# Cross-attention on one core: exponentials turned before the maxima, and the last output step moved to the following round

## The chip, the core and the metric

The kernel runs on one core of one Trainium2 chip. Its time is the device time of one execution in microseconds (us). Three executions of the kernel before took 1427.91, 1429.44 and 1430.26 us; the median is 1429.44 us.

## What is computed

There are 64 items; `x[b]` has 256 rows of 512 features, `c[b]` 256 rows of 384. All numbers are float32.

```python
text_p  = x @ W_text + b_text                      # 256 x 512
audio_p = c @ W_audio + b_audio                    # 256 x 512, also the values V
Q = layer_norm(text_p, g1, beta1)
K = layer_norm(audio_p, g2, beta2)
alpha = softmax(Q @ K.T / sqrt(512))
H = (alpha @ audio_p) @ W_out + b_out
out = layer_norm(H + x, g_out, beta_out)
```

The kernel folds W_audio and W_out into one matrix `wao` at the start, so that the last two products become (alpha @ c) @ wao, and b_audio, W_out and b_out into one row `bao`.

## The kernel before, in words

The program is one long unrolled list; each engine executes its own instructions in the order in which the source issues them, and no scheduler reorders them. The engines wait for each other through semaphores only where one reads or overwrites what another wrote.

**Rounds.** A main loop of 62 rounds (`for b in range(B - 2)`) works on five items at once. In round b, `k2` and `q2` are the projections of item b+2, `at` is the attention of item b, `last` that of b-1, `old` that of b-2 and `settled` that of b-3. A prologue projects items 0 and 1 and prepares the weights; a drain after the loop finishes the last items. 

**Products.** Each product of 256 rows is cut into blocks and computed with fewer block products than usual, at the price of sums. `Thirds` (key projection, and output `o`) makes 15 block products of 172 columns in the banks M, L, TU and N; `Fork` (query projection) makes seven of 256 columns in two banks, of which a part (`q2`) is cleared by `Fork.clear` (VectorE memset, L599) and another set by `Fork.seed` (ScalarE copy, L595). Between groups of products VectorE adds banks to each other (`after_one`, `after_three`, `after_four`, `after_five`, `after_six`: L538 to L561 and helper line L486), and later products wait for that. The sums of the left operands are made by GpSimd: `csum` and `zsum` in `Sides` (L320), `xsum` in `sum_x` (L288 to L291). `Sides.add(n)` issues the next n of its seven sums.

**Attention of an item.** `score` (TensorE, L672), `maxima` (VectorE, L682), `exponentials` (ScalarE, L689), `reciprocals` (VectorE, L699), `divide_e` (ScalarE, L703), `store_e` (to DRAM, L707). A round later `fetch_e` reads the exponentials back as 32x32 squares (four DMAs, L72), and `turn_e` transposes the squares on VectorE into `eT` (L75). `context_one` and `context_two` multiply `eT` by the rows of c (TensorE, L738) into `ps_z1` and `ps_z2`; `copy_one` and `copy_two` (ScalarE, L753 and L756) make `zT` of them, from which GpSimd makes `zsum`, and `o` multiplies by `wao`.

**End of an item.** `leave_plus` (VectorE, L486) adds the banks of `o` and x into the rows `y` (tile `yr`). A round later come `sums` and `deviations` (ScalarE, L782 and L790), the reciprocal deviation `rstd` on GpSimd (L372 and L376), and on VectorE `shift(0)`, `shift(1)` (L897), `settle(0)`, `settle(1)` (L906); `store` (L916) writes the 256 rows out. `shift` and `settle` read two operands from SBUF.

**Queues.** All loads and stores but two are issued by SyncE (SP), in program order; an issue that waits holds up those behind it. The order in a round before: `load_c`, `load_x` of item b+4, `fetch_e`, c rows, x rows, then the stores of q, of `y` (L916) and of k (L448), the fetches of q and k, the store of e.

**VectorE in a round before, from the end of `o`'s `after_four`:** `settle(1)`, `maxima`, `Fork.clear`, `turn_e`, `leave_plus` with `reciprocals` in its midst; then in the next round `after_one`, the turn of c, `after_three` (L543, twice L486), `after_six` (twice L486), `after_four`, `shift(0)`, `after_five` of q, `shift(1)`, `settle(0)`, the end of k, the turns of q and k, `after_one` of `o`, the turn of x, `after_three` and `after_four` of `o`.

Of the kernel before, what the change touches and what calls it, by code (L numbers as in the profile page):

```python
# [9 lines left out]
F32 = mybir.dt.float32  # L10
# [12 lines left out]
def kernel(  # L23
# [56 lines left out]
    def load_c(b):  # L80
        cq = blk.tile([P, S // SQ, DA // NQ], F32, tag="cq", name=f"cq_{b}")
        squares(cq, c[b])
        blocks[b] = [cq]

    def load_x(b):
        xq = blk.tile([P, L // SQ, D // NQ], F32, tag="xq", name=f"xq_{b}")
        squares(xq, x[b])
        blocks[b].append(xq)
# [5 lines left out]
    def load_x_rows(b):  # L94
        x_rows[b] = xin.tile([P, LT, D], F32, tag="x", name=f"x_{b}")
        nc.sync.dma_start(x_rows[b], x[b].rearrange("(t p) d -> p t d", p=P))

    def load_c_rows(b):
        c_rows[b] = cin.tile([P, ST, DA], F32, tag="c", name=f"c_{b}")
        nc.sync.dma_start(c_rows[b], c[b].rearrange("(t p) d -> p t d", p=P))  # L100
# [142 lines left out]
    def fold_bias(part):  # L243

        ps = third[3]
        nc.tensor.matmul(ps, lhsT=ones, rhs=part, start=True, stop=True)
        nc.vector.tensor_copy(bao_sb, ps)

    def moments(mv, src, t):

# [31 lines left out]
    def sum_x(xT):  # L282

        n = DC // 2
        part = lambda i, j: xT[:, j * n : (j + 1) * n, bass.ts(i, P)]
        s = work.tile([P, 4, n, P], F32, tag="xsum", name="xsum")
        add = nc.gpsimd.tensor_tensor
        add(s[:, 0], part(1, 0), part(1, 1), ALU.add)  # L288
        add(s[:, 1], s[:, 0], part(0, 0), ALU.subtract)  # L289
        add(s[:, 2], part(0, 0), part(1, 0), ALU.subtract)  # L290
        add(s[:, 3], part(0, 1), s[:, 1], ALU.subtract)  # L291
        ss = {
            1: part(0, 0), 2: part(0, 1), 4: part(1, 1),
            5: s[:, 0], 6: s[:, 1], 7: s[:, 2], 3: s[:, 3],
        }
        return {p: [ap[:, k, :] for k in range(n)] for p, ap in ss.items()}
# [624 lines left out]
    def turn_x(b):  # L921
        xT = work.tile([P, DC, L], F32, tag="xT", name=f"xT_{b}")
        turn(xT, blocks[b][1], DC)
        return xT
# [63 lines left out]
    k[1].evict(0)  # L988
    k[1].evict(1)
    Fork.clear()  # L990
    bt_step = const.tile([P, H2], F32, tag="bt_step", name="bt_step")
    nc.vector.tensor_tensor(bt_step, bt_sb[:, :H2], bt_sb[:, H2:], ALU.subtract)
    q[0].normalise()
    q[0].store()
    load_c(2)
    q[0].fetch()
    load_x(2)
    xT[1] = turn_x(1)
    Fork.seed()
    k[1].square()  # L1000
    xs[1] = sum_x(xT.pop(1))
# [27 lines left out]
    q[0].turn()  # L1029
    cT[2] = turn_c(2)  # L1030
    cs[2] = Sides(cT.pop(2), "csum").add()
    xT[2] = turn_x(2)
    xs[2] = sum_x(xT.pop(2))
    fold_multiply(2, 2, 4)
    fold_evict(2)
    q[0].affine(g1_sb, be1_sb)
    q[1].five()
    q[1].after_five()
    third_weights(wa_sb, wa_t, [1], nc.vector)
    fold_bias(part)  # L1040
    q[1].rest()
# [11 lines left out]
    def last_rows(b):  # L1053
        x_rows[b] = blk.tile([P, LT, D], F32, tag="xq", name=f"x_{b}")
        nc.sync.dma_start(x_rows[b], x[b].rearrange("(t p) d -> p t d", p=P))
        c_rows[b] = blk.tile([P, ST, DA], F32, tag="cq", name=f"c_{b}")
        nc.sync.dma_start(c_rows[b], c[b].rearrange("(t p) d -> p t d", p=P))

    for b in range(B - 2):
        at = att[b] = att.get(b) or Attention(b)  # L1060
        settled, old, last = att.pop(b - 3, None), att.get(b - 2), att.get(b - 1)
        three = b + 3 < B
        if b + 4 < B:
            load_c(b + 4)
            load_x(b + 4)
        if b > 1:
            last.fetch_e()
            load_c_rows(b)
            load_x_rows(b - 1)
        if not three:  # L1070
            last_rows(B - 2)
            last_rows(B - 1)
        if b == 1:
            go_sb = row(g_out, "go")
            beo_sb = row(beta_out, "beo")
        if b == 0:
            at.score(0, 8)
            Fork.seed()
            Fork.clear()
        k2 = k[b + 2] = Thirds("k", b + 2, cs.pop(b + 2), wa_blocks, ba_sb, ba_delta)  # L1080
        if b < 3:
            q[b + 2] = Fork(b + 2, xs.pop(b + 2), wt_blocks)
        q2 = q[b + 2]
        if settled:
            settled.sums()
        k2.one()
        k2.after_one()
        if b == 1:
            last.reciprocals()
            last.divide_e()  # L1090
            last.store_e()
            last.fetch_e()
            load_c_rows(b)
        k2.two()
        if old:
            old.context_two(0)
            old.context_two(1)
            old.copy_two()
        k2.three()
        if three:  # L1100
            cT[b + 3] = turn_c(b + 3)
        if b:
            at.affine_keys(0, 1)
        k2.after_three()
        if old:
            old.start_products()
        if b < 3:
            q2.one()
            q2.after_one()
        q2.seven()  # L1110
        q2.after_seven()
        if b:
            at.affine_keys(2, 3)
        q2.six()
        q2.after_six()
        if settled:
            settled.deviations()
        if three:
            cs[b + 3] = Sides(cT.pop(b + 3), "csum").add(2)
        k2.four()  # L1120
        k2.after_four()
        if settled:
            settled.shift(0)
        q2.five()
        q2.after_five()
        if settled:
            settled.shift(1)
            settled.settle(0)
        if b:
            at.affine_queries(0, 1)  # L1130
        k2.five()
        k2.after_five()
        k2.leave()
        k2.last_middle()
        if three:
            cs[b + 3].add(3)
        if old:
            old.o.seed()
        elif three:
            k2.seed()  # L1140
        if b:
            at.affine_queries(2, 3)
        q2.rest()
        q2.square()
        q2.scales()
        q[b + 1].turn()
        k[b + 1].turn([0])
        k2.square()
        k2.scales()
        if b:  # L1150
            at.score(0, 2)
        if old:
            old.o.one()
            old.o.after_one()
            old.o.two()
        if three:
            xT[b + 3] = turn_x(b + 3)
        if b:
            at.score(2, 4)
        if old:  # L1160
            old.o.three()
            old.o.after_three()
        k[b + 1].turn([1])
        if b:
            at.score(4, 7)
        if not three:
            att[b + 1] = Attention(b + 1)
            att[b + 1].affine_queries()
        q2.normalise()
        q2.store()  # L1170
        if old:
            old.o.four()
            old.o.after_four()
        if settled:
            settled.settle(1)
            settled.store()
        if b:
            at.score(7, 8)
        if old:
            old.o.five()  # L1180
        if three:
            Fork.seed()
        k2.normalise()
        k2.store()
        q2.fetch()
        k2.fetch()
        if three:
            cs[b + 3].add()
            xs[b + 3] = sum_x(xT.pop(b + 3))
        if b < 2:  # L1190
            wao_blocks = third_weights(wao_sb, wao_t, [b])
        if b == 1:
            last.turn_e()
        at.maxima()
        if three:
            Fork.clear()
        if not three:
            att[b + 1].affine_keys()
        at.exponentials()
        if b > 1:  # L1200
            last.turn_e()
        if three and b > 1:
            q3 = q[b + 3] = Fork(b + 3, xs.pop(b + 3), wt_blocks)
            q3.one()
            q3.after_one()
        if old:
            old.o.leave_plus(x_rows[b - 2], at.reciprocals)
        elif b:
            at.reciprocals()
        if last:  # L1210
            last.context_one()
        if three and old:
            k2.seed()
        if b:
            at.divide_e()
        if three and b:
            at.store_e()
        if last:
            last.copy_one()

    settled, old, last = att[B - 5], att[B - 4], att[B - 3]
    at = att[B - 2]
    load_x_rows(B - 3)
    for t in range(ST):
        old.context_two(t)
    old.copy_two()
# [3 lines left out]
    last.transpose_e(bank[4])  # L1230
    settled.statistics()
    last.copy_e()
    k[B - 1].turn()
    q[B - 1].turn()
    at.maxima()
    at.exponentials()
    at.reciprocals()
    old.o.one()
    old.o.after_one()
    settled.shift(0)  # L1240
    settled.shift(1)
    old.o.two()
    last.context_one()
    last.copy_one()
    old.o.three()
    old.o.after_three()
    for t in range(ST):
        last.context_two(t)
    last.copy_two()
# [102 lines left out]
```

## Time and profile before

| what | value |
|---|---|
| median of three runs | 1429.44 us |
| the profiled execution | 1432.0 us, span of its instructions 1430.2 us, mean granted TensorE clock 0.992 |
| busy share of the span | TensorE 98%, its weight loads 87%, VectorE 84%, ScalarE 77%, GpSimd 71% |
| a round in the middle (605.00 to 626.27 us) | 21.27 us, TensorE busy 21.24, VectorE 18.66, GpSimd 15.73 |
| the first 100 us | TensorE busy 83.78 us |
| 1370 to 1430.2 us | TensorE busy 43.23 us |

Times within the profile are microseconds from the start of the span. PE is TensorE's matmuls, PEld its weight loads (they run beside the matmul before), DVE is VectorE, ACT ScalarE, POOL GpSimd, SPq SyncE's queue. A float32 matmul appears as two instructions with a weight load each. A busy TensorE in the profile is not TensorE at its peak, since the ends of pipelined matmuls are modelled; a short wait is seen better in the distance between starts. A line of the timeline gives start, length, engine, line and tile, and in brackets the idle time of that engine just before with what ended it. A line of the windows gives, for a stretch, its length, then for PE, PEld, DVE, ACT and POOL the busy time with the number of instructions, then the granted clock, the share of DMA and GB/s.

### The profile page before, as it was taken

Reading aid. Unit: us, or ns where it says so; the run is one execution under the profiler, and the core shown is the slowest. Engines: PE = TensorE matmul, PEld = TensorE weight load, DVE = VectorE, ACT = ScalarE, POOL = GpSimd, SP = SyncE. Lnnn points to the kernel's source line nnn. Section 1 sums busy time; section 2 is a strip of 40 time slices with the busy share of each in tenths; the row PEclk is TensorE's granted clock in tenths of the full one; section 3 lists DMA queues with packets and bytes.
Section 4 is the critical chain, followed back from the end, with each engine's and each line's share of the span. In section 5 each row is a group of like instructions: output and inputs, shape, how many; then the busy total and the mean of one; then the engine's idle time right before and its main releaser. Section 6 shows DMA issues by size and latency. Waiting matters only on the chain.

```text
span 1430.2 us, 26034 instructions
## 1 busy us (share of the span) xinstructions
PE 1394.9 (98%) x7423; PEld 1240.5 (87%) x7423; DVE 1203.5 (84%) x2560; ACT 1100.7 (77%) x2814; POOL 1017.9 (71%) x1685
## 2 busy tenths in 40 slices
PE   9789999999999999999999999999999999999986
PEld 4679989999999899899898899898898999999874
DVE  5748888888888888888888988888888888888857
ACT  4558778778788788788787887887878878878863
POOL 3776877877877777777777787787787687777634
PEclk9989999999999999999999999999999999999999
DMA  8587787888788788787878878788878788777651
GB/s 212 144 212 220 226 245 235 228 237 243 231 229 248 233 238 235 233 232 231 242 227 244 234 226 248 232 230 238 240 226 238 244 229 242 236 233 228 209 174 74
DMA packets 449093, 321.99 MB, mean 225 GB/s; under 512 B 153781, under 2 KB 381621, under 8 KB 448950
## 3 DMA queue, kind: packets, MB, share of 16 engines
q1 hardware_dynamic: 448854, 320.20, 77.2%
q8 instruction: 60, 0.98, 0.3%
q14 instruction: 83, 0.68, 0.1%
q10 hardware_dynamic: 96, 0.13, 0.0%
HBM read 203.57 MB, written 116.65 MB: 224 GB/s over the span
## 4 chain that ended last, share of the span: by engine, by line
PE 82%; DMA 5%; POOL 3%; DVE 3%; SPq 2%; ACT 2%; issue 1%; DVEq 0%; ACTq 0%; POOLq 0%
PE ps_f L603 23%; PE ps_m L502 14%; PE ps_sc L672 13%; PE ps_z L738 11%; PE ps_n L502 10%; PE ps_u L502 7%; PE ps_l L502 5%; SPq L72 2%; DMA kd<-kr 2%; DMA xq<-in_x_dram 1%; POOL csum L320 1%; DMA ed<-e 1%; DMA c<-in_ctx_dram 1%; POOL rstd L376 1%; POOL xsum L289 0%
## 5 line engine op out<-in xcount | busy, mean ns | idle before, releaser
L320 POOL TENSOR_TENSOR zsum<-zT 128x256 f32<-128x256 f32 x124 | 73.9, 596 | 284.7 <-ACT zT L756 271.6
L672 PE MATMUL ps_sc<-kT,qT 128*128 128x256 f32 x1024 | 260.9, 379 | 0.5 <-ACT zT L753 0.5
L320 POOL TENSOR_TENSOR zsum<-zsum,zT 128x256 f32<-128x256 f32 x310 | 196.0, 650 | 14.6
L672 PEld LDWEIGHTS ps_sc<-kT,qT 128*128 128x128 f32 x1024 | 186.5, 190 | 17.9 <-ACT zT L753 0.9
L738 PE MATMUL ps_z<-eT,c 128*128 128x256 f32 x768 | 195.0, 391 | 7.0 <-DVE eT L75 5.6
L320 POOL TENSOR_TENSOR csum<-csum,cT 128x256 f32<-128x256 f32 x310 | 192.4, 629 | 9.8
L603 PE MATMUL ps_f<-wtsum,xsum 128*128 128x256 f32 x756 | 186.7, 383 | 0.9 <-POOL xsum L290 0.9
L906 DVE SCALAR_TENSOR_TENSOR yr<-yr,rstd,beo 128x512 f32<-128x512 f32 x124 | 131.4, 1061 | 52.0 <-POOL rstd L376 52.0
L738 PEld LDWEIGHTS ps_z<-eT,c 128*128 128x128 f32 x768 | 139.8, 192 | 36.3 <-DVE eT L75 20.4
L603 PEld LDWEIGHTS ps_f<-wtsum,xsum 128*128 128x128 f32 x756 | 139.3, 192 | 17.1 <-POOL xsum L290 1.7
L376 POOL TENSOR_TENSOR rstd<-ve,nhalf 128x2 f32<-128x2 f32 x192 | 136.4, 710 | 16.0
L477 ACT ACTIVATE kT<-kT,columns 128x256 f32<-128x256 f32 x256 | 139.5, 595 | 0.0
L477 ACT ACTIVATE qT<-qT,columns 128x256 f32<-128x256 f32 x256 | 138.8, 592 | 0.0
L603 PE MATMUL ps_f<-wt,xT 128*128 128x256 f32 x504 | 130.2, 381 | 0.0
L689 ACT ACTIVATE e<-ps_sc,nmx 128x256 f32<-128x256 f32 x128 | 59.6, 470 | 81.1 <-DVE nmx L682 81.1
L897 DVE SCALAR_TENSOR_TENSOR yr<-yr,nm,go 128x512 f32<-128x512 f32 x124 | 103.3, 835 | 0.0
L603 PEld LDWEIGHTS ps_f<-wt,xT 128*128 128x128 f32 x504 | 93.5, 191 | 10.2 <-issue 0.3
L486 DVE TENSOR_TENSOR ps_l<-ps_m,t 128x172 f32<-128x172 f32 x248 | 85.7, 346 | 17.3 <-ACT junk L410 0.5
L782 ACT ACTIVATE junk<-yr 128x512 f32<-128x512 f32 x124 | 77.0, 621 | 28.8 <-DVE yr L486 28.6
L486 DVE TENSOR_TENSOR ps_f<-ps_f,s 128x256 f32<-128x256 f32 x126 | 54.5, 432 | 49.7 <-PE ps_f L603 46.8
L561 ACT COPY kr<-ps_l 128x344 f32<-128x344 f32 x62 | 27.7, 446 | 87.0 <-DVE kr L486 86.7
L790 ACT ACTIVATE junk<-yr,nm 128x512 f32<-128x512 f32 x124 | 87.8, 712 | 0.0
(227 smaller groups left out, 3767.5 us busy)
## 6 DMA issues: line engine op xcount, KB each, us to landing
kd<-kr SPq DMA_DIRECT2D x64, 512.0 KB, 4.1
kq<-kd SPq DMA_DIRECT2D x256, 128.0 KB, 3.3
qd<-qr SPq DMA_DIRECT2D x64, 512.0 KB, 3.0
qq<-qd SPq DMA_DIRECT2D x256, 128.0 KB, 3.4
xq<-in_x_dram SPq DMA_DIRECT2D x252, 128.0 KB, 3.3
x<-in_x_dram SPq DMA_DIRECT2D x63, 512.0 KB, 4.4
out_dram<-yr SPq DMA_DIRECT2D x62, 512.0 KB, 2.8
cq<-in_ctx_dram SPq DMA_DIRECT2D x252, 96.0 KB, 3.5
```

Of the source, the lines that this page charges most:

```text
L320: nc.gpsimd.tensor_tensor(*step)
L376: nc.gpsimd.tensor_tensor(r, ve, nhalf[:, :n], ALU.pow)
L477: nc.scalar.activation(self.T[:, k, :], self.T[:, k, :], AF.Identity, bias=bet[:, k : k + 1], scale=gam[:, k : k + 1],)
L486: nc.vector.tensor_tensor(o, i0, i1, op)
L502: nc.tensor.matmul(place, lhsT=self.sides.of[n], rhs=self.weights[n], start=(n == 14), stop=True, skip_group_check=True,)
L603: nc.tensor.matmul(place, lhsT=side, rhs=w, start=False, stop=True, skip_group_check=True)
L672: nc.tensor.matmul(self.sc[:, t, :], lhsT=self.qT[:, k, bass.ts(t, P)], rhs=self.kT[:, k, :], start=(k == 0), stop=(k == HC - 1),)
L738: nc.tensor.matmul(ps, lhsT=c_rows[self.b][:, s, bass.ts(j, P)], rhs=self.eT[:, s, :], start=(s == 0), stop=(s == ST - 1),)
L782: nc.scalar.activation(junk, self.y[:, t, :], AF.Identity, scale=-1.0 / D, accum_out=self.nm[:, t : t + 1])
L790: nc.scalar.activation(junk, self.y[:, t, :], AF.Square, bias=self.nm[:, t : t + 1], accum_out=self.ssq[:, t : t + 1],)
L897: nc.vector.scalar_tensor_tensor(row, row, self.nm[:, t : t + 1], go_sb, ALU.add, ALU.mult)
L906: nc.vector.scalar_tensor_tensor(self.y[:, t, :], self.y[:, t, :], self.r[t], beo_sb, ALU.mult, ALU.add)
```

## The change

It moves instructions; it adds and removes none but one, a copy that goes to another engine. TensorE's own order is the same in both kernels, and ScalarE's too but for that copy.

- In each round from b = 2 on, `turn_e` stands ahead of `maxima` instead of behind `exponentials`.
- `settle(1)` and the store of `y` leave the end of the round; they come half a round later, in the next round, between `after_seven` and `six` of q (`done` carries the item over). On VectorE `settle(1)` then stands between `after_three` of k and `after_six` of q.
- `fetch_e` and the loads of c rows and x rows move from the head of the round to behind that store.
- Round 0 and 1: `Fork.clear` comes behind `after_one` of k; five instead of two of the sums `csum` come before `four`; in round 1 the store of e goes ahead of the loads of c and x of item 5, and the rows g_out and beta_out are loaded a round later.
- Prologue: `bt_step` behind the turn of x of item 1; the turn and sums of x of item 2 behind `after_five` of q; `bao` copied by ScalarE instead of VectorE.
- Drain: the turns of the last item's k and q go behind `after_three` of `old.o`, `reciprocals` a little later; the last `settle(1)` left over and its store come first.

```diff
@@ fold_bias
-        nc.vector.tensor_copy(bao_sb, ps)
+        nc.scalar.copy(bao_sb, ps)
@@ prologue
-    bt_step = const.tile([P, H2], F32, tag="bt_step", name="bt_step")
-    nc.vector.tensor_tensor(bt_step, bt_sb[:, :H2], bt_sb[:, H2:], ALU.subtract)
     q[0].normalise()
     q[0].store()
     load_c(2)
     q[0].fetch()
     load_x(2)
     xT[1] = turn_x(1)
+    bt_step = const.tile([P, H2], F32, tag="bt_step", name="bt_step")
+    nc.vector.tensor_tensor(bt_step, bt_sb[:, :H2], bt_sb[:, H2:], ALU.subtract)
     Fork.seed()
...
-    xT[2] = turn_x(2)
-    xs[2] = sum_x(xT.pop(2))
     fold_multiply(2, 2, 4)
     fold_evict(2)
     q[0].affine(g1_sb, be1_sb)
     q[1].five()
     q[1].after_five()
+    xT[2] = turn_x(2)
+    xs[2] = sum_x(xT.pop(2))
     third_weights(wa_sb, wa_t, [1], nc.vector)
@@ main loop
+    done = None
     for b in range(B - 2):
...
-        if b + 4 < B:
+        if b + 4 < B and b != 1:
             load_c(b + 4)
             load_x(b + 4)
-        if b > 1:
-            last.fetch_e()
-            load_c_rows(b)
-            load_x_rows(b - 1)
-        if not three:
-            last_rows(B - 2)
-            last_rows(B - 1)
-        if b == 1:
+        if b == 2:
             go_sb = row(g_out, "go")
             beo_sb = row(beta_out, "beo")
         if b == 0:
             at.score(0, 8)
             Fork.seed()
-            Fork.clear()
...
         k2.one()
         k2.after_one()
+        if b < 2:
+            Fork.clear()
         if b == 1:
             last.reciprocals()
             last.divide_e()
             last.store_e()
+            load_c(b + 4)
             last.fetch_e()
             load_c_rows(b)
+            load_x(b + 4)
         k2.two()
...
         q2.after_seven()
         if b:
             at.affine_keys(2, 3)
+        if done:
+            done.settle(1)
+            done.store()
+        done = settled
+        if b > 1:
+            last.fetch_e()
+            load_c_rows(b)
+            load_x_rows(b - 1)
+        if not three:
+            last_rows(B - 2)
+            last_rows(B - 1)
         q2.six()
         q2.after_six()
...
-            cs[b + 3] = Sides(cT.pop(b + 3), "csum").add(2)
+            cs[b + 3] = Sides(cT.pop(b + 3), "csum").add(2 if b > 1 else 5)
...
-            cs[b + 3].add(3)
+            cs[b + 3].add(3 if b > 1 else 0)
...
             old.o.four()
             old.o.after_four()
-        if settled:
-            settled.settle(1)
-            settled.store()
+        if last:
+            last.turn_e()
...
-        if b == 1:
-            last.turn_e()
         at.maxima()
-        if three:
+        if three and b:
             Fork.clear()
...
         at.exponentials()
-        if b > 1:
-            last.turn_e()
@@ drain
     load_x_rows(B - 3)
+    done.settle(1)
+    done.store()
...
     last.copy_e()
-    k[B - 1].turn()
-    q[B - 1].turn()
     at.maxima()
     at.exponentials()
-    at.reciprocals()
     old.o.one()
     old.o.after_one()
     settled.shift(0)
     settled.shift(1)
     old.o.two()
+    at.reciprocals()
     last.context_one()
     last.copy_one()
     old.o.three()
     old.o.after_three()
+    k[B - 1].turn()
+    q[B - 1].turn()
     for t in range(ST):
         last.context_two(t)
```

## The prediction

> **What bounds the kernel now.** I first read the windows, which say how full TensorE is in each stretch. Two of rounds:
>
> ```profile
> 605.00:626.27 21.27, 21.24 (x118) 19.23 (x117) 18.66 (x41) 17.16 (x45) 15.73 (x27) 1.00 0.80 237
> 626.27:647.54 21.27, 21.24 (x118) 19.23 (x117) 18.66 (x41) 17.16 (x45) 15.73 (x27) 1.00 0.82 235
> 116.04:136.93 20.89, 20.89 (x117) 19.20 (x115) 18.21 (x40) 17.08 (x44) 15.35 (x26) 1.00 0.71 199
> ```
>
> TensorE is full in the middle, so little can be had there: yet the first full round takes 20.89 us and the later ones 21.27. It is the one round whose context product finds `eT` ready, because `settle(1)` does not yet stand ahead of `maxima`. The timeline shows the 0.38 us in a later round:
>
> ```profile
> 604.27 0.68 DVE L75 STREAM_TRANSPOSE eT<-eq 128x512 f32<-128x512 f32 x1
> 605.00 1.59 PEld L738 LDWEIGHTS ps_z<-eT,c 128*128 128x128 f32 x8 [0.24 <-DVE eT L75]
> 606.37 0.52 DVE L486 TENSOR_TENSOR yr<-ps_n,n 128x344 f32<-128x344 f32 x1
> 607.00 0.59 PEld L502 LDWEIGHTS ps_n<-wa,csum 128*128 128x128 f32 x4 [0.40 <-issue]
> ```
>
> The context waits for `eT`; then the next key product waits until `leave_plus` has read bank N (606.89), and that is late because the turn of `eT` stood ahead of it. The remaining idle time is at the ends: TensorE works 83.78 of the first 100 us and 43.23 of the last 60. Its waits there, with what stood behind them:
>
> ```profile
> 53.98 0.27 DVE L599 MEMSET ps_f<- 128x256 f32 x1 [3.08 <-ACT qr L652]
> 55.00 0.91 PE L502 MATMUL ps_u<-wa_thirds,csum 128*128 128x172 f32 x2 [2.55 <-DVE ps_u L486]
> 92.77 3.46 PE L738 MATMUL ps_z<-eT,c 128*128 128x256 f32 x8 [5.40 <-DVE eT L75]
> 1386.93 0.91 PE L502 MATMUL ps_u<-wao_thirds,zsum 128*128 128x172 f32 x2 [4.61 <-DVE ps_u L486]
> ```
> ```profile
> 81.87 0.38 SPq L707 DMA_DIRECT2D ed<-e  x1
> 88.57 1.81 SPq L72 DMA_DIRECT2D eq<-ed  x4
> ```
> ```profile
> 1381.97 1.25 DVE L75 STREAM_TRANSPOSE kT<-kq 128x1024 f32<-128x1024 f32 x1 [6.22 <-DMA kq<-kd]
> ```
>
> **The drain.** VectorE waits 6.22 us for `kq`; `maxima` and `after_one`, which frees TensorE, stand behind. With the turns moved, `maxima` runs when the scores end (about 1379.1) and bank T is written at 1380.7, so the product of 1386.93 follows the context directly, at 1382.2: 4.8 us. The granted clock was 0.5 from 1386.0 to 1392.8; the products from 1386.93 to 1392.96 took 6.03 us, at the full-clock pitch of the loop (146 and 216 ns a pass) 3.05. Without the idle time that is 3.0 more. What is late next: both turns (1.25 and 1.20) plus one `settle` (0.74) now stand ahead of `after_four`, which ends near 1387.4, where the next product into M could start at 1385.8: 1.8 back. `settle(1)` at the head is hidden in VectorE's wait for scores. ScalarE's affines (4.1 us) end before they are needed. `kq` should land earlier, as no store precedes that of k; were it as late as before (1381.9), the turns, due at 1383.7, would still not wait. Gain 4.8 + 3.0 - 1.8 = **6.0**, bounds 3 (half clock again) to 7.8 (no 1.8).
>
> **The start.** Round 0: the memset waits for `qr`, `after_one` behind it. Turned round, bank T is ready when VectorE's weight sums end (about 51), and the next wait is that for the query bank's seed (ScalarE, 53.74 to 54.12): the query product starts at 54.2, not 55.71, 1.5. `bt_step` (1.18) behind the turn lets GpSimd's chain, without a pause from 33.46 to the `rstd` of 52.55, start up to 1.1 sooner; `bao` (0.68) goes where ScalarE is idle. I take 2.0, between 1.5 and 2.6. Round 1: the query product at 72.18 waits for squares, `rstd`, `csum`, `xsum` in a row, which stay; the earlier sums and the clear gain nothing: 0. Then the store of e: it was ready at 72.9, but queued behind the fetches of q and k and ten loads. Now it follows the fetch of k, which ends at 76.86, 5.0 earlier, with one load (1.9) before its fetch; even with its landing of 6.7 the fetch is issued by 83.6 rather than 88.57, with the median 3.6 by 80.6. `eT` is then there about 84 to 87, and the scores ended at 87.37: the wait of 5.40 goes, and the half clock behind it (3.46 against 1.73): 7.1. Late next is GpSimd: `wao_thirds` runs to 96.4 and had 2.4 us before `zsum`; with all earlier by nine, `zsum` waits for it. The output product is due 12 us after the context, so this costs 0 to 1.5; I take 0.6. Loads put off (x of item 5, g_out, beta_out) have over 10 us until use. Sum 2.0 + 7.1 - 0.6 = **8.5**, bounds 5 and 11.
>
> **The rounds.** `turn_e` (0.61 from start to start) takes the place of `settle(1)` (0.87): `maxima` 0.26 sooner, `leave_plus` 0.6 more by the turn that no longer stands behind it. Both waits vanish: -0.38, the row of 20.89. The cover of the fetch: it is issued some 0.5 us later or as before, as the k store no longer waits for `y` (603.95 to about 603.05), lands about 620, is turned at 623.7; c and x rows have over 2 us too. Behind `settle(1)` in its new place stand `after_six` and GpSimd's `zsum`. After `after_three` VectorE had 0.63 idle; `settle` needs more, because it meets `zsum`. The price is shown where `settle(0)` meets `csum`:
>
> ```profile
> 615.70 0.73 POOL L320 TENSOR_TENSOR csum<-cT 128x256 f32<-128x256 f32 x1
> 615.77 1.20 DVE L906 SCALAR_TENSOR_TENSOR yr<-yr,rstd,beo 128x512 f32<-128x512 f32 x1 [0.87 <-POOL rstd L376]
> 616.51 1.06 POOL L320 TENSOR_TENSOR csum<-csum,cT 128x256 f32<-128x256 f32 x1
> ```
>
> The later of the two is held until the earlier is nearly done: `settle` ends 0.55 after `csum`, alone it takes 0.74; the next `csum` loses 0.33. In the new place the second `zsum` (610.59) starts 0.11 ahead of `settle` (610.70): the same order. `settle` then takes 1.16, `after_six` ends 0.35 later, the query product behind it is late by 0.14; hidden, because a longer chain comes: `zsum` 0.33 later, `rstd` too, then `settle(0)` (which already waits 0.87 for it), the end of k, the turns, `after_three` of `o` at 622.18, without a gap. That was on TensorE's heels: its load came at 622.24, 0.06 late within the 20.89. So 20.89 + 0.33 = 21.22 against 21.27: **-0.05** a round, 57 rounds, 2.7 us. Bounds: -0.38 (GpSimd had slack I do not see) to +0.53 (below).
>
> The Trainium skill (SBUF — State Buffer, "Who interferes with whom") speaks against this step: a VectorE instruction with two SBUF inputs and a GpSimd one that reads SBUF exclude each other for the whole instruction. By its letter the third `zsum` would lose not the row's 0.33 but some 0.66, and the rounds would cost 0.28 each, 16 us, nearly all that the ends give. The rows go against the letter, and I go by them.
>
> **Sum.** 8.5 + 2.7 + 6.0 = 17.2. The profiled execution took 1432.0 (span 1430.2): 1414.8 by it. It stands 2.6 above the median of 1429.44, from which the same 17.2 gives **1412**.
>
> For the clock, the trace shows half speed from 54.81 after an idle stretch of 2.55, and from 71.88 after idle stretches of 0.63, 2.23 and 0.28. The Trainium skill (TensorE: Matmul & The Clock Gate, "Why this matters for your kernels") asks only that gaps stay under some 3 us. By it no gap left at the start would halve the clock, and 5 us more would go; by the trace gaps of 2 us in close order suffice, so I count none of it.
>
> **Rivals.**
> 1. *The rounds keep the whole 0.38.* For it: 20.89 was reached with both shifts and `settle(0)` in place. Against: there `settle(1)` did not meet `zsum`. 57 x 0.38 = 21.7 with 14.5 at the ends: 1393.
> 2. *The ends give half.* The half clock returns, GpSimd is late in round 2, `kq` lands late: 8 in all for 14.5, 2.7 in the rounds: 1419; without the rounds' share 1422.
> 3. *Slower: `settle(1)` gets ahead of the second `zsum`.* The margin is 0.11 us. Then that `zsum` ends 0.7 later, the shifts hold two more, and `rstd` comes 0.9 later: 20.89 + 0.9 = 21.8, +0.53 a round, 30 us against 14.5: 1445. It decides from a chain over 0.63 late (0.38 + 14.5 / 57). For it: the small margin; against: in 615.70 / 615.77 GpSimd goes first by 0.07, in every round.
> 4. *The change does not do what it says:* the fetch lands too late for the earlier turn, and the wait only changes its place; at 0.1 more a round (5.7) and half of the ends' gain (7.2), 1428.
>
> **How the numbers follow.** Forecast 0.52 (1404 to 1417), rival 1 0.13, rival 2 0.18, rival 3 0.12, rival 4 0.05. About 0.2% (2.9 us) can be told from no change. Faster 0.83, same 0.05, slower 0.12. The range takes in the forecast with its bounds, rival 2 and the near part of rival 1: 1398 to 1426.
>
> **What would show it.** Right: no wait over 1 us near 87 and near 1383, context starts 21.2 apart, PEld waits for `eT` gone, a POOL row of about 1.06 in `zsum`, VectorE's wait for `rstd` still there. Wrong: starts 21.5 or more apart, `after_six` or L906 of 1.5 us, or rounds of 20.9; a new wait of TensorE for `zsum` in round 2.

## The result and the profile after

The changed kernel takes 1410.27 us (median of four runs, 1409.14 to 1412.36), the kernel before 1429.08 beside it: a ratio of 0.987, interval 0.9853 to 0.9887. The profiled execution took 1412.36 us, its span 1410.6. Forecast were 1412 and a range of 1398 to 1426. The total was right; two of its three terms were over 2 us off.

A round in the middle, from the windows of the changed kernel (columns as before: length, busy times of PE, PEld, DVE, ACT and POOL, clock, DMA share, GB/s):

```profile
605.00:626.20 21.20, 21.20 (x118) 19.30 (x117) 19.05 (x41) 17.04 (x46) 15.71 (x27) 1.00 0.81 237
```

21.20 instead of 21.27, and VectorE is busy 0.39 us longer than before, though it does the same work. The timeline of the changed kernel shows where:

```profile
608.14 0.59 PEld L502 LDWEIGHTS ps_m<-wao_thirds,zsum 128*128 128x128 f32 x4 [0.25 <-DVE ps_l L486]
...
617.39 3.68 POOL L320 TENSOR_TENSOR zsum<-zsum,zT 128x256 f32<-128x256 f32 x5
617.50 1.17 DVE L906 SCALAR_TENSOR_TENSOR yr<-yr,rstd,beo 128x512 f32<-128x512 f32 x1
618.58 0.42 DVE L486 TENSOR_TENSOR ps_f<-ps_f,s 128x256 f32<-128x256 f32 x1
...
622.89 1.20 DVE L906 SCALAR_TENSOR_TENSOR yr<-yr,rstd,beo 128x512 f32<-128x512 f32 x1 [0.87 <-POOL rstd L376]
```

`settle(1)` starts 0.11 behind the second `zsum` and takes 1.17; the five sums take 3.68; the first settle still waits 0.87 for `rstd`. The load into M waits 0.25 us for `after_three` of `o`. In the waits of the changed kernel (engine, line, what for: us in total, times, longest) TensorE's loads no longer wait for `eT` (20.4 us in 59 times before); two others took its place:

```profile
PEld ps_m L502 <- DVE ps_l L486: 14.1, 57, 0.2
PEld ps_u L502 <- POOL csum L320: 11.8, 57, 2.6
```

The start, in the timeline of the changed kernel:

```profile
71.97 0.40 SPq L707 DMA_DIRECT2D ed<-e  x1
75.65 1.79 SPq L72 DMA_DIRECT2D eq<-ed  x4
79.58 0.67 DVE L75 STREAM_TRANSPOSE eT<-eq 128x512 f32<-128x512 f32 x1
80.83 1.89 PE L738 MATMUL ps_z<-eT,c 128*128 128x256 f32 x8
```

The store of e was at 81.87, its fetch at 88.57, the context at 92.77 behind a wait of 5.40 and at half clock (3.46). Now all of it is 10 to 13 us earlier, the wait is gone and the product runs at full clock (1.89).

The drain, in TensorE's timeline:

```profile
1358.80 5.41 PE L672 MATMUL ps_sc<-kT,qT 128*128 128x256 f32 x16 [0.48 <-ACT zT L753]
...
1367.38 0.46 PE L502 MATMUL ps_u<-wao_thirds,zsum 128*128 128x172 f32 x2
...
1372.55 0.85 PE L502 MATMUL ps_m<-wao_thirds,zT 128*128 128x172 f32 x4 [1.38 <-DVE ps_u L486]
...
1396.20 4.54 PE L807 MATMUL ps_m<-wao,zT 128*128 128x512 f32 x6 [2.23 <-ACT zT L753]
```

The wait of 4.61 is gone, 1.38 came as the next one. But the 16 scores took 5.41 instead of 3.72, and the last product of six passes 4.54 instead of 2.84: half clock again, elsewhere.

To see where the time lies, I cut every profiled span at the starts of two context products: that of round 3 and that of the last round of the loop, round 61 (58 rounds between).

| profiled execution | to round 3 | 58 rounds | from there to the end | half clock in the first 100 us |
|---|---|---|---|---|
| before | 136.93 | 1234.11 | 59.17 | 13.65 |
| after | 124.45 | 1229.65 | 56.47 | 3.41 |
| e1_start | 124.82 | 1233.84 | 57.72 | 6.82 |
| e2_loop | 133.84 | 1230.16 | 56.71 | 10.24 |
| e3_drain | 137.03 | 1234.04 | 54.31 | 20.49 |
| e4_swap | 125.31 | 1211.11 | 54.66 | 6.82 |
| e5_turn_late | 125.95 | 1230.42 | 54.67 | 6.83 |
| e6_turn_only | 126.69 | 1233.24 | 53.38 | 6.83 |
| e7_filler | 125.71 | 1211.12 | 54.48 | 6.83 |
| e8_all | 127.66 | 1211.20 | 54.71 | 3.42 |
| e9_end | 125.04 | 1211.47 | 54.10 | 3.41 |
| e10_settle_first | 123.38 | 1221.31 | 54.67 | 0 |

The middle column repeats to 0.5 us for equal loops; the outer ones, of equal code, scatter by up to 3.3 us. One pair of profiles is not enough to price the ends.

In the changed kernel's profile some 0.65 us of the first column is the wait of rival 4, in one round only: the early turn waited 1.05 us for the fetched exponentials (at 101.52), and from the context of round 2 to that of round 3 it took 21.56 us instead of the 20.9 of most others. e9 lost 0.9 the same way (a wait of 1.31); the other versions with an early turn lost nothing there.

### The profile page after: what moved, and what is told of

It reads as the page before. It is cut to its first block, busy times and chain, and to the rows that moved or that the text cites. A ratio compares the mean times of both kernels' runs of the same rounds, so it can differ in the third digit from the quotient of the medians.

```text
span 1410.6 us, 26095 instructions
## 1 busy us (share of the span) xinstructions
PE 1388.2 (98%) x7423; PEld 1241.4 (88%) x7423; DVE 1225.0 (87%) x2559; ACT 1094.5 (78%) x2815; POOL 1017.5 (72%) x1685
## 4 chain that ended last, share of the span: by engine, by line
PE 91%; DVE 2%; ACT 2%; POOL 2%; issue 1%; DMA 1%; SPq 1%; DVEq 0%; ACTq 0%; POOLq 0%
PE ps_f L603 26%; PE ps_m L502 16%; PE ps_sc L672 14%; PE ps_z L738 11%; PE ps_n L502 10%; PE ps_u L502 7%; PE ps_l L502 5%; SPq L72 1%; POOL csum L320 0%; DMA eq<-ed 0%; PE ps_f L392 0%; ACT qr L652 0%; POOL zsum L320 0%; PE ps_m L807 0%; ACT qT L477 0%
## 5 line engine op out<-in xcount | busy, mean ns | idle before, releaser
L320 POOL TENSOR_TENSOR zsum<-zsum,zT 128x256 f32<-128x256 f32 x310 | 215.8, 714 | 14.6
L603 PE MATMUL ps_f<-wtsum,xsum 128*128 128x256 f32 x756 | 189.9, 387 | 1.7 <-DVE ps_f L486 1.4
L906 DVE SCALAR_TENSOR_TENSOR yr<-yr,rstd,beo 128x512 f32<-128x512 f32 x124 | 144.1, 1163 | 51.8 <-POOL rstd L376 51.8
L738 PE MATMUL ps_z<-eT,c 128*128 128x256 f32 x768 | 186.6, 379 | 1.9 <-ACT e L689 1.2
L738 PEld LDWEIGHTS ps_z<-eT,c 128*128 128x128 f32 x768 | 142.9, 190 | 19.1 <-ACT e L689 1.6
L603 PEld LDWEIGHTS ps_f<-wtsum,xsum 128*128 128x128 f32 x756 | 136.1, 190 | 22.2 <-DVE ps_f L486 2.2
L897 DVE SCALAR_TENSOR_TENSOR yr<-yr,nm,go 128x512 f32<-128x512 f32 x124 | 117.4, 949 | 0.0
L486 DVE TENSOR_TENSOR ps_l<-ps_m,t 128x172 f32<-128x172 f32 x248 | 85.7, 346 | 17.2 <-DVE t L543 0.5
L652 ACT ACTIVATE qr<-ps_f,rstd 128x512 f32<-128x512 f32 x126 | 79.7, 683 | 6.1 <-POOL rstd L376 6.1
L438 ACT ACTIVATE kr<-kr,rstd 128x512 f32<-128x512 f32 x126 | 84.1, 720 | 0.0
```

The source lines that it names most:

```text
L320: nc.gpsimd.tensor_tensor(*step)
L438: nc.scalar.mul(row, row, self.r[t])
L486: nc.vector.tensor_tensor(o, i0, i1, op)
L603: nc.tensor.matmul(place, lhsT=side, rhs=w, start=False, stop=True, skip_group_check=True)
L738: nc.tensor.matmul(ps, lhsT=c_rows[self.b][:, s, bass.ts(j, P)], rhs=self.eT[:, s, :], start=(s == 0), stop=(s == ST - 1),)
L897: nc.vector.scalar_tensor_tensor(row, row, self.nm[:, t : t + 1], go_sb, ALU.add, ALU.mult)
```

## The experiments

My theory after the result: the rounds are bound as predicted, by `settle(1)` meeting `zsum`; the ends were won in waits and in half-clock time, of which the start gave more and the drain less than I had counted. First each part alone on the kernel before.

**e1_start.** The edits of the prologue and of rounds 0 and 1:

```diff
+        if b < 2:
+            Fork.clear()
         if b == 1:
             last.reciprocals()
             last.divide_e()
             last.store_e()
+            load_c(b + 4)
             last.fetch_e()
...
-            cs[b + 3] = Sides(cT.pop(b + 3), "csum").add(2)
+            cs[b + 3] = Sides(cT.pop(b + 3), "csum").add(2 if b > 1 else 5)
```

> The kernel before with the edits of the prologue and of rounds 0 and 1 alone. Theory (from the two traces: 12.5 us by the context product of round 2, of which some 5 us are half-clock time that is gone, and the rest waits): 1417 us, 12.5 less than before, context starts 21.27 apart in the later rounds and a last round as before. My recorded step (8.5, two of the three half-clock windows left as they were): 1421. Rival, that the start gains only together with the loop's new order, because the first rounds would wait for VectorE again: 1423 or more.

1418.27 us, ratio 0.9931 (0.9916 to 0.9946): 10.2 less than the 1428.51 beside it, between my recorded 8.5 and the 12.5 of the single pair of traces. The start does not need the new loop.

**e2_loop.** The loop's edits from round 2 on:

```diff
+        if done:
+            done.settle(1)
+            done.store()
+        done = settled
...
-        if settled:
-            settled.settle(1)
-            settled.store()
+        if last:
+            last.turn_e()
```

> The kernel before with the edits of the loop from round 2 on alone (the turn of e ahead of the maxima, the second settle and the store half a round later, the fetch of e and the row loads behind them). Theory (58 rounds at 0.06 to 0.08 each by the traces): 1425 us, 4.0 to 4.5 less than before, starts 21.20 apart. My recorded step: 2.7 less, 1426.7. Rival, that the rounds owe their gain to the earlier start (transfers that land sooner) and not to the order: 21.27 and 1429.

1422.31 us, ratio 0.9957 (0.9943 to 0.9972), 6.2 less. The 58 rounds gave 4.0 (table), as expected, on the start of the kernel before: its starts are 21.20 to 21.23 apart, so the rounds owe nothing to the earlier start. The drain gave 1.0 (against e1) to 2.5 (against before), though of its edits only the left-over settle and its store at the head are in: in this profile `kq` is turned 9.68 us after the last round's context instead of 10.92, and the wait of 4.61 is 2.88. No store of `y` stands between those of q and k any more, and the store of k lands 2.9 us after its issue instead of 6.7. That part I had not expected.

**e3_drain.** The turns of k and q behind `after_three`, the reciprocals later:

```diff
-    k[B - 1].turn()
-    q[B - 1].turn()
     at.maxima()
     at.exponentials()
...
     old.o.after_three()
+    k[B - 1].turn()
+    q[B - 1].turn()
```

> The kernel before with the drain's edits alone (turns of k and q behind the third evict, reciprocals later). Theory (the wait of 4.61 goes, but the half clock does not go, it comes in other windows): 2.7 less, 1426.7 us, and still two or more half-clock windows in the last 60 us. My recorded step: 6.0 less, 1423.4, with no half clock in the score products. Rival, that the drain's edits need the second settle to have been put off: no gain, 1429.

1424.79 us, ratio 0.9975 (0.9966 to 0.9985), 3.7 less, between the two. Its profile has one half-clock stretch in the drain ahead of the final one, at the last product. The three parts sum to 20.1, the whole gave 18.8. The 1.3 between them lie within the intervals; they would fit e2 and e3 each taking away part of the same wait.

**e4_swap.** The test of the bound. `settle(1)` and the turn of c change places:

```diff
         k2.three()
-        if three:
-            cT[b + 3] = turn_c(b + 3)
+        if done:
+            done.settle(1)
+            done.store()
+        done = settled
...
-        if done:
-            done.settle(1)
-            done.store()
-        done = settled
+        if three:
+            cT[b + 3] = turn_c(b + 3)
```

> The changed kernel with the second settle (and its store) and the turn of c put in each other's place: the settle stands behind the first evict of k, where GpSimd is idle for 4 us, and the turn of c, which is one input only, meets the zsum. Same work. Theory (the round is bound by settle meeting zsum, which makes zsum 0.33 late, then rstd, the first settle, and the third evict of the output): L906 there 0.74 instead of 1.17, zsum x5 3.35 instead of 3.68, starts 20.90 apart, 17 us less than the changed kernel: about 1393. Rival, that the round is bound by something else (the first settle's own meeting with csum, or VectorE's load of 87%): starts 21.15 to 21.22 and 1407 to 1411. Rival that the settle in front of the turn of c makes the second evict of k late: slower, 21.4 and 1420.

1392.75 us, ratio 0.9753 (0.9737 to 0.9769), what the theory said. The timeline and the window of this kernel:

```profile
608.97 0.74 DVE L906 SCALAR_TENSOR_TENSOR yr<-yr,rstd,beo 128x512 f32<-128x512 f32 x1
...
611.05 3.35 POOL L320 TENSOR_TENSOR zsum<-zsum,zT 128x256 f32<-128x256 f32 x5
611.15 0.97 DVE L75 STREAM_TRANSPOSE cT<-cq 128x768 f32<-128x768 f32 x1
```

```profile
605.65:626.53 20.88, 20.88 (x118) 19.38 (x117) 18.44 (x41) 17.04 (x44) 15.34 (x27) 1.00 0.83 239
```

Alone the settle takes 0.74, the sums 3.35 beside the turn, which reads one input. The round is 20.88, and neither TensorE nor its loads wait for anything in it. The 0.33 us of the meeting were the whole distance.

TensorE's products come in the same order in the kernel before, in the changed one and in e4, so their starts can be laid side by side. Against a round of e4, one of the changed kernel loses 0.09 us at the query product behind `after_six`, 0.03 at a product of `o` and 0.20 at the one into M behind `after_three` of `o`: 0.32 in all. One of the kernel before loses 0.10 at the context and 0.27 at the key product into N.

**e5_turn_late** and **e6_turn_only** take the loop's two moves apart. In e5 `turn_e` goes back behind `exponentials` (from round 2 on):

```diff
-        if last:
+        if b == 1:
             last.turn_e()
...
         at.exponentials()
+        if b > 1:
+            last.turn_e()
```

> The changed kernel with the turn of e back behind the exponentials (from round 2 on); the second settle stays half a round later. Theory (it is the settle, 0.87 us, that stood in the way; without it the turn ends some 0.7 us ahead of the context product either way, and the output's last evict starts at the same time): no change, rounds of 21.20 to 21.22, 1409 to 1412 us. Rival, that the turn's own move brings the gain: the wait of 0.24 of the context for eT is back, rounds 21.35 to 21.45, 1419 to 1425.

1411.17 us, ratio 0.9869 (0.9847 to 0.9892); rounds of 21.20 to 21.22: no change, as the theory had it. In e6 `turn_e` stays early and the settle goes to the round's end, into the old place of the turn (the drain's `done` lines go too):

```diff
-        if done:
-            done.settle(1)
-            done.store()
-        done = settled
...
         at.exponentials()
+        if settled:
+            settled.settle(1)
+            settled.store()
```

> The changed kernel with the second settle and its store at the round's end again, behind the exponentials, where the turn of e stood before; the turn stays ahead of the maxima. Theory: the context's wait for eT is gone, but the settle now keeps the output's last evict late, so the next key product waits 0.4 us or more for bank N, the more as GpSimd's xsum runs beside the settle; zsum takes its 3.35 again. Rounds of 21.1 to 21.35, 1405 to 1419, most likely 21.3 and 1416. Rival, that the turn's move alone is worth it: 20.9 and 1393.

1414.88 us, ratio 0.9895 (0.9874 to 0.9916); rounds of 21.25 to 21.30, those of before. Its timeline, where one wait has only gone into the other:

```profile
614.97 0.93 DVE L906 SCALAR_TENSOR_TENSOR yr<-yr,rstd,beo 128x512 f32<-128x512 f32 x1
615.31 1.19 POOL L291 TENSOR_TENSOR xsum<-xT,xsum 128x256 f32<-128x256 f32 x1
...
615.83 0.50 DVE L486 TENSOR_TENSOR n<-ps_m,x 128x344 f32<-128x344 f32 x1
...
617.98 0.59 PEld L502 LDWEIGHTS ps_n<-wa,csum 128*128 128x128 f32 x4 [0.52 <-issue]
```

The context follows without a wait for `eT`; the load of the next key product waits 0.52 for bank N instead of 0.40, and by the starts of the products all of the 0.39 lost against e4 is there. So the title's first half, the turn ahead of the maxima, brings nothing in either run: not beside the moved settle (e5), and not with the settle in the turn's old place (e6). The gain of the rounds is the settle's move out of the stretch ahead of `leave_plus`.

**e10_settle_first.** What if VectorE goes first, as in rival 3? From the changed kernel, the settle behind the turn of c:

```diff
         if three:
             cT[b + 3] = turn_c(b + 3)
+        if done:
+            done.settle(1)
+            done.store()
+        done = settled
```

> The changed kernel with the second settle right behind the turn of c, ahead of the third evict of k, so that the settle starts some 0.3 us ahead of GpSimd's first zsum instead of 0.11 behind its second: the case of rival 3, in which VectorE goes first. By what the rows show of the pair (the one held ends as if it had started shortly before the other's end), the first zsum ends 0.3 late and the rest runs free: zsum as late as in the changed kernel, rounds of 21.2, and the third evict 0.65 late on top, which TensorE meets or not: 21.2 to 21.6, 1410 to 1433. By the price that rival 3 has in the prediction (zsum 0.7 late, rstd 0.9): 21.8 and 1445. If the pair costs GpSimd nothing in this order: 20.9 and 1393.

1400.99 us, ratio 0.9817 (0.9792 to 0.9841). Some 21.06 a round, between the 20.9 of no cost and the 21.2 of my first sum. Its timeline:

```profile
612.00 0.71 DVE L906 SCALAR_TENSOR_TENSOR yr<-yr,rstd,beo 128x512 f32<-128x512 f32 x1
612.38 0.92 POOL L320 TENSOR_TENSOR zsum<-zT 128x256 f32<-128x256 f32 x1 [4.34 <-ACT zT L756]
...
613.38 3.35 POOL L320 TENSOR_TENSOR zsum<-zsum,zT 128x256 f32<-128x256 f32 x5
```

The first sum, begun 0.33 before the settle's end, takes 0.92 instead of 0.73: 0.19 lost. Against e4 the round is 0.18 longer, all of it at the product into M behind `after_three` of `o`. The later evict costs TensorE nothing.

**e7_filler.** Matmuls without use in the last wait, to test the clock, on e4:

```diff
     end.context()
+    keep_busy(18)
     at.shift(1)
```

> The version with settle and the turn of c exchanged (median 1392.75), with 18 more matmuls of 128x128 of ones into a bank that nobody reads, in the wait of 2.25 us ahead of the last output product; nothing else moves. Theory (the granted clock falls to half for one 3.41-us stretch after a stretch in which TensorE was idle over some 60%; 2.25 of 3.41 was, so it is the filler's time that keeps the clock): the product of six passes takes 2.84 instead of 4.54 and the whole is 1.7 us shorter, 1391. Rival, that the half clock comes from something else (the load, or the end of the program): 4.54 stays and 1392.75 too.

1392.60 us, ratio 0.9742 (0.9716 to 0.9769): no gain, though in the profiled execution the last product ran at full clock. TensorE's timeline of e4, then that of e7:

```profile
1376.72 4.54 PE L807 MATMUL ps_m<-wao,zT 128*128 128x512 f32 x6 [2.25 <-ACT zT L753]
```

```profile
1372.03 2.86 PE L738 MATMUL ps_z<-eT,c 128*128 128x256 f32 x12 [0.68 <-ACT eT L727]
1374.72 4.18 PE L180 MATMUL ps_f<-ones 128*128 128x128 f32 x36
1378.74 2.74 PE L807 MATMUL ps_m<-wao,zT 128*128 128x512 f32 x6
```

I had the filler too long: a float32 matmul is two instructions, 36 of them took 4.18 for a wait of 2.25, so the product began some 1.6 later, as seen from the context (6.71 against 5.11), and took 1.8 less. Nor does the run show that the filler kept the clock. In this execution the wait without the filler would have left its stretch of 3.41 us idle for some 51%, a share behind which the clock fell in some cases and not in others (last section), and four executions with the same wait and no filler (before, e1, e2, e6) ran the product at full clock too.

**e8_all.** e4 with four edits at the ends; the cores of three (the fourth moves the loads of g_out and beta_out behind the fetch of e in round 2):

```diff
-            cs[b + 3] = Sides(cT.pop(b + 3), "csum").add(2 if b > 1 else 5)
+            cs[b + 3] = Sides(cT.pop(b + 3), "csum").add(2 if b > 1 else 7)
...
         if b == 1:
+            last.maxima()
+            last.exponentials()
+            at.k.turn([1])
             last.reciprocals()
...
     old.o.after_four()
+    q[B - 1].turn()
     settled.settle(1)
...
-    last.statistics()
     end.context()
+    last.statistics()
```

> The best version the traces suggest: settle and the turn of c exchanged (1392.75), and four small edits at the ends. Round 0: all sums of c at once, and maxima, exponentials and half a turn of k put off behind the first evict of round 1, for the wait of 2.35 us before the first product of round 1 (theory: 1.3 less, and 1.7 more if the half clock goes with it). The loads of g_out and beta_out behind the fetch of e in round 2 (0 to 0.4). The turn of q in the drain behind the fourth evict (0.8). The last context's copies ahead of the output statistics on ScalarE (1.7, and 1.7 more as the half clock of the last product goes). Sum 4 to 7.5: 1385 to 1389 us. Rival, that GpSimd (xsum behind the norms) and the input of the scores hold the start, and the end is held by statistics that now come later: 1391 or more.

1392.04 us, ratio 0.974 (0.9715 to 0.9765): my sum of 4 to 7.5 is not there. In round 1 waits of 1.10, 0.65, 0.70 and 1.59 (released by GpSimd, by the seed, by xsum and by ScalarE's evict) stand in place of the 2.35 and 0.70 of e4. At the end the last product runs without a gap and at full clock, but from the last context product to the end it is 19.64 us as against 19.47 in e4: ScalarE's statistics, and with them VectorE's shifts and settles, are later, and the last evicts stand behind those.

**e9_end.** So on e4 only the end, with VectorE's evicts ahead:

```diff
-    last.statistics()
     end.context()
+    last.statistics()
...
+    end.evict(0, stats=False)
+    end.statistics(0, 1)
     last.shift(0)
     last.shift(1)
-    last.settle(0)
-    last.settle(1)
-    last.store()
-    end.evict(0, stats=False)
-    end.statistics(0, 1)
```

(the settles and the store follow behind the last `shift(1)`.)

> The exchange of settle and the turn of c (1392.75 us) with one more edit at the very end: the last context's copies ahead of the statistics of the output before it on ScalarE, and on VectorE the last output's evicts ahead of the shifts and settles of the one before. Theory: the last output products follow the context with a gap of 0.5 instead of 2.25 and at the full clock (3.4 less), of which the chain behind them, VectorE's 13 instructions up to the last store, keeps some 1.2; from the last context product to the last instruction 17.3 instead of 19.5, so 2.2 less, 1390.5 us. Rival, that the end is held by VectorE's sum of work whatever the order: 1392 to 1393.

1392.11 us, ratio 0.9748 (0.973 to 0.9765): not to be told from e4. From the last context product to the end 18.90 instead of 19.47; VectorE works nearly without a pause from the first evict to the last settle, the rival's case. None of the three versions built on e4 can be told from it. The best version is thus e4, one exchange away from the changed kernel and about 17 us faster than it (1392.75 against 1428.51 for the kernel before beside it, where the changed kernel had 1410.27 against 1429.08).

## Why the prediction was right, and where not

**The rounds: right in mechanism, size and sign.** Predicted were 21.22 a round, a settle of 1.16, `zsum` 0.33 late, `after_three` of `o` late for TensorE's load, and the wait for `rstd` still there; measured 21.20, 1.17, 0.33 (3.68 against 3.35), 0.25 of wait at that load, and 0.87. e4 takes the meeting away and gets 20.88, the row of 20.89 I had started from. 58 rounds gave 4.0 to 4.5 us, not 2.7 (57 times 0.05 would have been 2.9): 0.065 a round in the steady part, and 0.6 in the last two rounds, which I had not looked at.

One reading in this step was loose: I let the turn's move and the settle's move share in the 0.38. In e5 the turn stands ahead of `leave_plus` as before, and the key product does not wait: it was the settle that stood in the way.

**The Trainium skill's rule** (SBUF — State Buffer, "Who interferes with whom") holds for who is hit: the settle with two SBUF inputs collides with GpSimd's sums (e4 without, after with), the turn of c with one input does not (3.35 beside it). What it says of the shared port pair, "an exclusive lock", gives too high a price here: 0.33 us lost in the changed kernel where the prediction had some 0.66 by the letter, and 0.19 in e10, where the letter gives 0.33 (the overlap with the settle). The rows were the better guide.

**Rival 3** was priced too high, as far as the runs go. In the one case that I ran with VectorE first, ahead of the first `zsum` and not of the second, the sum loses 0.19 and the round 0.18, not 0.9: faster than the changed kernel, not slower. Its own case, the settle ahead of the second `zsum`, did not occur and was not run.

**The start: the term for the clock was too small.** I counted 8.5, of which 1.7 for half clock behind the wait for `eT`, "so I count none of it" for the rest. The three starts of the old code come to 135.9 us on average (context of round 3), the eight of the new code (all the others but e8) to 125.2: 10.8 less. Half-clock time in the first 100 us falls on average from 14.8 to 5.1 us, worth at most half of the difference, 4.8. That leaves some 6.0 for the waits, against my 6.8; this split is an estimate from means, not a measurement. The give-back of 0.6 did not come: `zsum` of round 2 does start directly behind `wao_thirds`, at 89.99, but no product waits for it. The rule that speaks of gaps under some 3 us (TensorE: Matmul & The Clock Gate, "Why this matters for your kernels") would have made it 13.5; what was measured lies in the middle. Against the rule, the clock halved in the changed kernel (from 65.62) around a gap of 2.35 us in round 1's key product; for it, e10 kept the full clock behind the same wait.

**The drain: the sum of 6.0 read the clock off one execution.** The wait went as predicted: in e5, whose drain is that of the changed kernel, the product that waited 4.61 follows 11.51 us after the last round's context instead of 15.88 (4.4; predicted 4.8), and 1.37 comes back as a wait for M (predicted 1.8). The clock did not. From that product to the last context e5 takes 23.72 us, the kernel before 25.07: 1.35 less, as the 3.0 - 1.8 had it. But e1, which has the drain of the kernel before, takes 23.70: its half clock there lasted 3.41 us (from 1374.17), not 6.83, and by this pair nothing is gained. From the last context to the end e5 takes 19.44, before 18.22, e1 18.21, because e5's last product runs at half clock. That is not shown to be a price of the change: behind a wait of 2.23 to 2.26 us, which old and new code share, the last product took 4.54 us in five profiles (after, e3, e4, e5, e10) and 2.84 in four (before, e1, e2, e6). In the changed kernel's profile a half-clock stretch fell on the scores too, for 1.7. The two drains of the old code took 59.17 and 57.72 (before, e1), the four of the new code 56.47, 54.66, 54.67 and 54.67 (after, e4, e5, e10): 3.3 less on average. The step that failed is "at the full-clock pitch ... 3.0 more": it takes the half clock of one execution for a cost of the code, and does not ask whether another stretch comes.

The errors, 2.3 too little at the start, some 1.5 too little in the rounds and some 2.7 too much in the drain, partly cancel: 17.2 forecast, 18.8 between the medians. That the total came closer than its terms is luck.

## What to carry to other kernels

When an instruction has to be moved off a chain, ask first which other engine reads SBUF at the new place: the move to a spot where GpSimd sums was worth 0.07 us a round, the move to a spot where it waits for its input 0.39. Price each move of a change by itself, since one of them can bring nothing. And at the ends of a kernel take the mean of several executions: the same code there scattered by 3.3 us at the start and by 1.8 in the drain.

## What the hardware showed beyond that

In each profile the changes of the clock lie whole multiples of 3.413 us apart (before: 54.81, 58.22, 71.88 and so on); where this grid begins differs from execution to execution. The Trainium skill (TensorE: Matmul & The Clock Gate, "Part 1: The HAM clock gate") names a free-running window of some 3.4 us; it asks for one that is idle before the clock halves, and these runs show that less is enough. I laid this grid over TensorE's rows of all twelve profiles, from 44 us on. Of the full-clock stretches, all 28 in which TensorE was idle 59.8% or more were followed by half clock, none of the 35 with 25 to 47%, and 9 of the 17 between (49 to 59%). Equal waits then cost 0 or 1.7 us by where the grid falls. Two windows each of e5 and e6, around the same wait of 2.23 us ahead of the last product:

```profile
1394.04:1397.45 3.41, 1.18 (x4) 0.50 (x4) 3.00 (x6) 3.41 (x11) 2.08 (x3) 1.00 0.00 0
1397.45:1400.86 3.41, 3.41 (x5) 1.33 (x4) 2.40 (x2) 0.08 (x1) 1.44 (x2) 0.50 0.32 118
```

```profile
1395.99:1399.40 3.41, 1.99 (x10) 1.41 (x8) 3.27 (x8) 2.45 (x7) 0.68 (x1) 1.00 0.01 4
1399.40:1402.81 3.41, 2.60 (x6) 1.25 (x7) 2.82 (x3) 1.65 (x5) 2.85 (x4) 1.00 0.01 2
```

The first column after the length is TensorE's busy time, the clock stands third from the end. In e5 the wait falls into one stretch (1.18 us busy), the next runs at 0.50, and the product takes 4.54; in e6 an edge of the grid cuts the wait in two (1.99 and 2.60 busy), the clock stays, and the product takes 2.84. Two things stay open: what decides between 49 and 59%, and why some half-clock stretches last twice as long (71.88 to 78.70 before, where the first of the two was 92% busy).
